# Feed-forward products of a pre-norm delta-rule block: seven-product float32 scheme replaced by two one-pass halves with integer weights, behind a check of the weights

## The chip, the core and the metric

The kernel runs on one core of one Trainium2 chip. The core has five engines that work side by side: TensorE (PE in the profile, with its weight loads shown apart as PEld), VectorE (DVE), ScalarE (ACT), GpSimd (POOL) and SyncE (SP), which here issues nearly all DMA transfers. The metric is the device time of one execution in microseconds (us). The kernel before takes 2001.05 us, the median of three runs (1995.74 to 2001.29).

## The reference

32 sequences of 512 tokens with 256 features, float32. A layer norm is followed by the attention block (a second layer norm, keys normalised to unit length, a triangular solve with the keys' Gram matrix, an answer from queries and keys, then an MLP with ReLU), and that by a gated feed-forward block whose weights are int32 numbers times 1/127. Only the last part is changed:

```python
def _L0_ffn_ref(x, w_gate, w_up, w_down):        # x: 32 x 512 x 256
    SCALE = 1.0 / 127.0
    wg = w_gate.astype(x.dtype) * SCALE          # 768 x 256, integers from -127 to 127
    wu = w_up.astype(x.dtype) * SCALE            # 768 x 256
    wd = w_down.astype(x.dtype) * SCALE          # 256 x 768
    gate = jnp.einsum('bsd,hd->bsh', x, wg)
    up = jnp.einsum('bsd,hd->bsh', x, wu)
    h = jax.nn.silu(gate) * up
    return jnp.einsum('bsh,dh->bsd', h, wd)
...
x = x + _L0_attn_ref(_layernorm(x), ...)
x = x + _L0_ffn_ref(_layernorm(x), w_gate, w_up, w_down)
```

## The kernel before

**Pairs and phases.** The 32 sequences are worked on in 16 pairs; in the code a pair is `one, two`. The order of every engine's instructions is the order in which the Python program emits them (`tc.manual_schedule`), so an instruction that waits holds up everything behind it on its engine. In the steady state the program goes round three phases, and each works on up to three pairs at once:

- the **values phase** (`values_phase`) of the newest pair: `gather` (tile `pf`), `through_values` (`pz`), `through_keys` (`pm`), `answer` (`po_d`), the layer norm `normed(s, "m")`. Beside it VectorE runs the inversion of the next pair's diagonal blocks (`invert`, lines 770 and 776), dealt out in small steps: each TensorE operation calls `spend(columns)`, and that moves each generator in `sides` on at its own rate;
- the **middle** (`middle`) of the pair before: the MLP (`mlp_in`, tile `pa`, line 1013; `mlp_out`, `po_m`, line 936), the layer norm `normed(s, "f")`, and between them the first steps of the newest pair's solve (`solution`: `merge` with tiles `pw` and `py`, then `solve` with `pr` and `pu`). `merge` starts with three VectorE transposes of the inverted blocks, which come back through DRAM (`found`, then `yb`, lines 785 and 791);
- the **gated phase** (the loop over `gated(old)`): the gate and up products of the feed-forward block for the pair before, the rest of the solve, the input norm of the next pair (`prepare`, which ends with a transpose by way of DRAM, `way_a` and `ag`, lines 502 to 515), and, from step `EARLY` on, the next pair's keys (`pk`, line 623) and Gram matrices (`pg`, line 665).

A transposed tile of a norm takes four DMAs out (`Turn.send`, line 509) and one back (`Turn.fetch`, line 515), all on SP's queue, in the order of the program.

**The feed-forward products.** Each is done by blocks of two by two in seven products in place of eight (a Strassen scheme in the form with few additions). `Unit` holds one pair of 128-row blocks of gate or up: seven float32 matmuls of 128x256 (line 1069) with weights that were combined once at the start (`wgS`, `wuS`, seven blocks for each of three pairs), with inputs combined by `mixed` on GpSimd (`hS`, line 1041). Results are put together by ScalarE copies (lines 1083, 1091, 1103), VectorE (1121, 1132, 1140) and GpSimd (1109, 1110, 1115, 1136). `Down` does the last product for half a sequence: three products at once (`plain`, `po_x`, line 1200), a recombination of the hidden values on GpSimd (`mix`, lines 1223 to 1226), then four more (`combined`, `po_y`), all of 128x128. `plain` and `combined` of a pair are spread over the values phase and the middle that follow its gated phase. A float32 product is two MATMUL instructions in the trace.

**PSUM.** Eight banks: `ps_a` has three, `ps_x` one, and `ps_f`, from which the MLP, the values phase and the feed-forward products take theirs, four.

The constants at the head set where things stand in the gated loop of 85 steps:

```python
NORM, STORE, START, TURN, MIX, EARLY = 3, 8, 13, 15, 28, 56
PREPARE = 14 * 1024
INVERT = 17 * 1024
```

Of the kernel before, what the change touches and what calls it, by code (L numbers as in the profile page):

```python
# [11 lines left out]
I32 = mybir.dt.int32  # L12
AF = mybir.ActivationFunctionType
# [5 lines left out]
WSCALE = 1.0 / 127.0  # L19


@with_exitstack
def kernel(
    ctx: ExitStack,
    tc: tile.TileContext,
    x: bass.AP,
# [28 lines left out]


# [10 lines left out]
    NORM, STORE, START, TURN, MIX, EARLY = 3, 8, 13, 15, 28, 56  # L67
    BEGIN = 17
    PREPARE = 14 * 1024
# [269 lines left out]
    NP = NH // 2  # L339
    wdS = const.tile([P, NP, 7, P], F32, name="wdS")  # L340

    wgS = const.tile([P, NP, 7, P], F32, name="wgS")
    wuS = const.tile([P, NP, 7, P], F32, name="wuS")

    class Dequant:
# [19 lines left out]
        def scale(self):  # L368
            for r0, m, wi in self.parts:
                nc.gpsimd.tensor_scalar(wi.bitcast(F32), wi, WSCALE, None, ALU.mult)  # L370

# [11 lines left out]
    class Stationary:  # L383


        def __init__(self, dst):
            self.dst = dst
            self.a21 = wk.tile([P, NP, P], F32, tag="fz", name="a21", bufs=4)

        def put(self, cc, r0, m, pt):  # L390
            dst, some = self.dst, slice(r0 // 2, (r0 + m) // 2)
            pt = pt.rearrange("p (j i r) -> p j i r", i=2, r=P)
            nc.scalar.copy(dst[:, some, cc, :], pt[:, :, 0, :])
            nc.scalar.copy(dst[:, some, 3, :] if cc else self.a21[:, some, :], pt[:, :, 1, :])
            if cc == NF - 1 and r0 + m == NH:
                b = lambda i: dst[:, :, i, :]
                two = lambda o, x, y, op: nc.gpsimd.tensor_tensor(o, x, y, op)
                two(b(4), self.a21, b(3), ALU.add)
                two(b(6), b(0), self.a21, ALU.subtract)
                two(b(5), b(4), b(0), ALU.subtract)  # L400
                two(b(2), b(1), b(5), ALU.subtract)

    class Combined:


        def __init__(self):
            self.b12 = wk.tile([P, NP, P], F32, tag="uv", name="b12", bufs=1)

        def put(self, cc, r0, m, pt):
            j, k = cc // 2, cc % 2  # L410
            nc.scalar.copy(wdS[:, j, k, :], pt[:, :P])
            nc.scalar.copy(wdS[:, j, 6, :] if k else self.b12[:, j, :], pt[:, P:])
            if cc == NH - 1:
                b = lambda i: wdS[:, :, i, :]
                minus = lambda o, x, y: nc.gpsimd.tensor_tensor(o, x, y, ALU.subtract)
                minus(b(5), self.b12, b(0))
                minus(b(3), b(6), b(5))
                minus(b(4), b(6), self.b12)
                minus(b(2), b(1), b(3))

# [613 lines left out]
    def mixed(s):  # L1034


        tag = {"tag": "ka"} if s.n % NS == 0 else {"tag": "blocks", "bufs": 1}
        hS = wk.tile([P, 4, T // 2], F32, name=f"hS_{s.n}", **tag)
        t1, t2, t3, t4 = [hS[:, i] for i in range(4)]
        block = lambda f, t: s.hT[:, f, t * (T // 2) : (t + 1) * (T // 2)]  # L1040
        minus = lambda o, x, y: nc.gpsimd.tensor_tensor(o, x, y, ALU.subtract)
        s.B = {
            1: block(0, 0), 2: block(1, 0), 3: block(1, 1), 4: t4, 5: t1,
            6: t2, 7: t3,
        }
        minus(t1, block(0, 1), block(0, 0))
        yield
        minus(t2, block(1, 1), t1)
        yield
# [3 lines left out]
        yield  # L1053

    class Unit:

# [120 lines left out]

    class Down:

# [526 lines left out]
```

## Time and profile before

| | |
|---|---|
| median of three runs | 2001.05 us |
| profiled execution, first to last instruction (span) | 1992.6 us |
| runs beyond that span (median; lowest run) | 8.5 us; 3.1 us |
| TensorE clock granted, mean | 0.997 of full speed |
| ACT busy | 873.0 us (44%), 2271 instructions |
| POOL busy | 1151.5 us (58%), 1556 instructions |
| DMA | 164.14 MB, mean 82 GB/s |
| gate and up products (`py`, `pz`, line 1069) | 2688 matmul instructions of 128x256 |
| down products (`po_x`, `po_y`, `po_z`, line 1200) | 2688 matmul instructions of 128x128 |
| starts of the values phases 1 to 14 | 200.3 us to 1771.1 us: 13 periods, mean 120.8 us |

The profile is one execution, with a row for each instruction. Busy time is the union of an engine's rows; a matmul's end is modelled, so the price of one in a stream is read from the distance of starts, not from its duration: 16 `pf` instructions of 128x256 start at 822.89 us and the next operation at 826.34, so each costs 0.216 us, while its row says 0.379.

### The profile page before, as it was taken

The page shows a single profiled execution, that of the slowest core. Times are in us where ns is not written, and L with a number is a line of the kernel's source. Part 1 is how long each engine was busy: PE and PEld are TensorE (multiplying, and loading weights), DVE is VectorE, ACT ScalarE, POOL GpSimd, SP SyncE. Part 2 cuts the span into 40 slices and gives each one's busy share as a digit, 9 for nine tenths or more (in the row PEclk, how much of TensorE's full clock was granted, in tenths as well). Part 3 has the DMA queues.
Part 4 walks back from the last instruction along what each step waited for, and adds up shares of the span by engine and source line. Part 5 has one row for each costly group of instructions (what it writes and reads, how often), then busy time and mean ns, then how long its engine had stood idle before and what let it go on. Part 6 is the DMA issues. An engine that isn't in the chain of part 4 may idle for free.

```text
span 1992.6 us, 31232 instructions
## 1 busy us (share of the span) xinstructions
PE 1955.4 (98%) x10286; PEld 1582.8 (79%) x10286; DVE 1337.8 (67%) x3873; ACT 873.0 (44%) x2271; POOL 1151.5 (58%) x1556
## 2 busy tenths in 40 slices
PE   7999999999999999999999999999999999999998
PEld 4667878878788787887878788787877878878888
DVE  6774875849668495784848758496684957758254
ACT  5345353453534435353453534535344353434543
POOL 3435764656555565664657645565555656646666
PEclk9999999999999999999999999999999999999999
DMA  5111242423424233241332324233242332413120
GB/s 151 39 35 44 74 117 51 133 64 82 117 59 112 67 104 86 63 120 53 104 86 74 116 56 130 68 78 116 59 112 67 103 87 63 128 45 103 43 64 22
DMA packets 248426, 164.14 MB, mean 82 GB/s; under 512 B 80929, under 2 KB 223912, under 8 KB 248264
## 3 DMA queue, kind: packets, MB, share of 16 engines
q1 hardware_dynamic: 247750, 161.61, 29.8%
q8 instruction: 82, 1.34, 0.3%
q14 instruction: 80, 0.66, 0.1%
q10 hardware_dynamic: 434, 0.39, 0.1%
q0 software_dynamic: 80, 0.14, 0.0%
HBM read 96.02 MB, written 66.06 MB: 81 GB/s over the span
## 4 chain that ended last, share of the span: by engine, by line
PE 77%; DVE 15%; DMA 3%; POOL 2%; issue 1%; ACT 1%; SPq 0%; DVEq 0%; ACTq 0%; POOLq 0%
PE po_y L1200 7%; PE pg L665 6%; PE pyup L1069 6%; PE pygate L1069 6%; PE pa L1013 5%; PE pk L623 5%; PE po_m L936 5%; PE po_x L1200 5%; PE po_d L936 5%; PE pr L874 4%; PE pzup L1069 4%; PE pf L895 4%; PE pzgate L1069 4%; PE pu L884 3%; PE pm L895 2%; PE pz L895 2%
## 5 line engine op out<-in xcount | busy, mean ns | idle before, releaser
L1109 POOL TENSOR_TENSOR v_up<-v_up,five_up 128x256 f32<-128x256 f32 x96 | 70.1, 730 | 217.0 <-ACT v_up L1083 216.9
L1200 PE MATMUL po_y<-wdS,hid 128*128 128x128 f32 x1512 | 180.6, 276 | 0.0
L1200 PEld LDWEIGHTS po_y<-wdS,hid 128*128 128x128 f32 x1512 | 177.3, 192 | 4.1 <-issue 1.0
L1132 DVE TENSOR_TENSOR top_up<-top_up,pzup 128x512 f32<-128x512 f32 x96 | 64.9, 676 | 164.1 <-PE pzup L1069 161.7
L1069 PE MATMUL pyup<-hS,wuS 128*128 128x256 f32 x576 | 172.8, 382 | 1.2
L1069 PE MATMUL pygate<-hS,wgS 128*128 128x256 f32 x576 | 171.5, 379 | 0.1
L665 PE MATMUL pg<-kT 128*128 128x256 f32 (+3 forms) x512 | 157.1, 433 | 0.1
L1140 DVE TENSOR_TENSOR hid<-top_gate,pzgate 128x512 f32<-128x512 f32 x96 | 64.6, 673 | 125.8 <-PE pzgate L1069 125.7
L1200 PEld LDWEIGHTS po_x<-wdS,hid 128*128 128x128 f32 x1152 | 138.4, 192 | 4.4 <-DVE hid L1136 1.2
L1200 PE MATMUL po_x<-wdS,hid 128*128 128x128 f32 x1152 | 138.9, 275 | 1.0 <-DVE hid L1136 1.0
L1115 POOL TENSOR_TENSOR hid<-v_gate,five_gate 128x256 f32<-128x256 f32 x96 | 69.9, 729 | 120.6 <-ACT v_gate L1083 120.6
L1069 PEld LDWEIGHTS pyup<-hS,wuS 128*128 128x128 f32 x576 | 106.7, 190 | 38.3 <-issue 13.4
L1069 PEld LDWEIGHTS pygate<-hS,wgS 128*128 128x128 f32 x576 | 108.7, 190 | 28.2 <-issue 13.6
L1136 POOL TENSOR_TENSOR hid<-hid,top_up 128x512 f32<-128x512 f32 x95 | 120.8, 1271 | 15.9 <-DVE top_up L1132 15.9
L936 PE MATMUL po_m<-w2s,act 128*128 128x256 f32 x512 | 123.6, 385 | 0.0
L623 PE MATMUL pk<-ag,wa 128*128 128x512 f32 x256 | 120.4, 595 | 1.7 <-ACT ag L485 0.9
L665 PEld LDWEIGHTS pg<-kT 128*128 128x128 f32 x512 | 91.9, 190 | 36.0 <-issue 12.9
L1013 PE MATMUL pa<-hT_m,w1s 128*128 128x512 f32 x256 | 118.8, 607 | 0.0
L895 PE MATMUL pf<-a,dp 128*128 128x256 f32 x512 | 115.6, 379 | 0.0
L1069 PE MATMUL pzup<-hT_f,wuS 128*128 128x256 f32 x384 | 114.5, 380 | 0.5 <-DVE a L1251 0.4
L1069 PE MATMUL pzgate<-hT_f,wgS 128*128 128x256 f32 x384 | 114.8, 381 | 0.0
L433 POOL TENSOR_TENSOR r_m<-ve_m,neghalf 128x4 f32<-128x4 f32 x32 | 32.7, 1023 | 139.8 <-DVE nmn_m L459 139.8
(273 smaller groups left out, 4882.0 us busy)
## 6 DMA issues: line engine op xcount, KB each, us to landing
a<-in_L_attn_x_dram SPq DMA_DIRECT2D x32, 512.0 KB, 4.6
x<-in_L_attn_x_dram SPq DMA_DIRECT2D x32, 512.0 KB, 4.0
way_m<-turn_m SPq DMA_DIRECT2D x120, 128.0 KB, 2.3
hT_m<-way_m SPq DMA_DIRECT2D x30, 512.0 KB, 3.7
out_dram<-a SPq DMA_DIRECT2D x60, 256.0 KB, 2.9
way_a<-turn_a SPq DMA_DIRECT2D x112, 128.0 KB, 2.3
ag<-way_a SPq DMA_DIRECT2D x28, 512.0 KB, 3.7
way_f<-turn_f SPq DMA_DIRECT2D x112, 128.0 KB, 2.4
```

Of the source, the lines that this page charges most:

```text
L623: nc.tensor.matmul(pk, lhsT=wa[:, f, ts(o, P)], rhs=s.ag[:, f, :], start=(f == 0), stop=(f == NF - 1),)
L665: nc.tensor.matmul(pg[:, :w], lhsT=s.kT[:, f, ts(j, P)], rhs=s.kT[:, f, j * P :], start=(f == 0), stop=(f == NF - 1),)
L874: nc.tensor.matmul(pr, lhsT=s.go[j][:, ts(i - j - 1, P)], rhs=p_[:, j, :], start=(j == 0), stop=(j == i - 1),)
L895: nc.tensor.matmul(s.pp[:, o, :], lhsT=lhs[:, c, ts(o, P)], rhs=rhs[:, c, :], start=(c == 0), stop=(c == nk - 1),)
L936: nc.tensor.matmul(self.po[:, c % 2, :], lhsT=src[:, ts(c, P)], rhs=self.w[:, f, :], start=(f == 0), stop=(f == self.nk - 1),)
L1013: nc.tensor.matmul(pa, lhsT=w1s[:, f, ts(o, P)], rhs=s.hT[:, f, :], start=(f == 0), stop=(f == NF - 1),)
L1069: nc.tensor.matmul(dst, lhsT=self.w[:, self.j, self.SLOT[i], :], rhs=self.s.B[i], start=first, stop=last, skip_group_check=True,)
L1109: nc.gpsimd.tensor_tensor(v, v, self.five, ALU.add)
L1115: nc.gpsimd.tensor_tensor(to, self.half(v), self.half(self.five), ALU.add)
L1132: nc.vector.tensor_tensor(self.top, self.top, self.z, ALU.add)
L1136: later(4, lambda: engine.tensor_tensor(natural(g), natural(g), grouped(flat(self.top)), ALU.mult))
L1200: nc.tensor.matmul(po[:, i, :], lhsT=self.A[block][:, j, :], rhs=wdS[:, j, slot, :], start=(j == 0), stop=(j == NP - 1),)
```

## The change

The constants, the weights and the halves. Weights stay integers (the multiplication by 1/127 becomes one by 1.0; `WSCALE` moves into the SiLU's scale and, squared, into the last addition). `float32r` (`FR`) is a type of the same four bytes. Inputs and hidden values are split into a rounded copy and what is left:

```diff
-    NORM, STORE, START, TURN, MIX, EARLY = 3, 8, 13, 15, 28, 56
-    PREPARE = 14 * 1024
+    NORM, TURN, SPLIT, EARLY = 2, 14, 24, 26
+    GATED, TAIL = 44, 12
+    PREPARE = 16 * 1024
...
+    W = FR if exact else F32
+    PARTS = 2 if exact else 1
+    wgT = const.tile([P, NF, HID], W, name="wgT")
...
+    def widest(sources):
...
+        for i, (r0, m, wi) in enumerate(parts):
+            wf = wi.bitcast(F32).rearrange("p r c -> p (r c)")
+            nc.vector.tensor_tensor_reduce(
+                out=wf, in0=wf, in1=wf, scale=1.0, scalar=0.0,
+                op0=ALU.mult, op1=ALU.max, accum_out=top[:, i : i + 1],
+            )
+        nc.vector.tensor_reduce(top[:, 0:1], top, axis=AX.X, op=ALU.max)
+        pt = ps_f.tile([P, 512], F32, tag="mm", name="pwide")
+        nc.tensor.transpose(pt[0:1, :P], top[:, 0:1], ident)
...
+        nc.vector.tensor_scalar(wide, most, EXACT * EXACT, None, ALU.is_gt)
...
+    def split(s, first, second):
...
+        parts = wk.tile([P, 2, NF, T], FR, tag="split", name=f"split_{s.n}")
+        for f in range(NF):
+            nc.scalar.copy(parts[:, 0, f, :], s.hT[:, f, :])
+        for f, engine in enumerate((first, second)):
+            engine.tensor_tensor(
+                parts[:, 1, f, :], s.hT[:, f, :], parts[:, 0, f, :], ALU.subtract
+            )
```

`mixed`, `Unit` and `Down` go; `Block` (128 rows of the hidden values of one sequence) takes their place. The down product of a block adds to two PSUM banks that stay taken over a sequence's six blocks:

```diff
+        def project(self, w, name):
+            po = ps_f.tile([P, 512], F32, tag="mm", name=f"p{name}_{self.name}")
+            for p, part in enumerate(self.s.parts):
+                for f in range(NF):
+                    nc.tensor.matmul(
+                        po, lhsT=w[:, f, ts(self.j, P)], rhs=part[:, f, :],
...
+                    if f == NF - 1 or not exact:
+                        yield
+            return po
...
+            nc.scalar.activation(natural(self.h), grouped(pg), AF.Silu, scale=WSCALE)
...
+            nc.vector.tensor_tensor(h, h, grouped(pu), ALU.mult)
+            if exact:
+                mine = self.hid()
+                hi, lo = mine[:, 0, :], mine[:, 1, :]
+                later(2, lambda: nc.scalar.copy(hi, self.h))
+                later(3, lambda: nc.gpsimd.tensor_tensor(lo, self.h, hi, ALU.subtract))
...
+        def down(self, half_):
+            s, j = self.s, self.j
+            if j == 0:
+                s.po[half_] = ps_f.tile([P, 2, C], F32, tag="mm", name=f"po_f_{s.n}_{half_}")
+            po = s.po[half_]
+            for i in range(2):
+                for p in range(PARTS):
+                    nc.tensor.matmul(
+                        po[:, i, :], lhsT=self.mine[:, p, ts(2 * half_ + i, P)],
+                        rhs=wdT[:, j, :], start=(j == 0 and i == 0 and p == 0),
...
+            if j == NH - 1:
+                nc.vector.scalar_tensor_tensor(
+                    out=acc, in0=po, scalar=WSCALE * WSCALE, in1=acc,
+                    op0=ALU.mult, op1=ALU.add,
+                )
+                nc.sync.dma_start(
...
+                    acc,
+                )
...
+    LAG = 2
...
+        for n in range(len(blocks) + LAG):
+            if n < len(blocks):
+                for part in (blocks[n].gate, blocks[n].up):
+                    for _ in part(later):
+                        step()
+                        yield
+            if n >= LAG:
+                for half_ in range(NT // 2):
+                    blocks[n - LAG].down(half_)
+                    step()
+                    yield
```

The gated loop runs 44 of these 72 steps; 12 more go to the end of the next values phase, 12 to the middle, the last 4 behind them (`older` is the same generator). The middle and the values phase in the new order:

```diff
+        mlp_in(one, 0)
+        mlp_in(one, 1)
+        residual(one)
+        sides_[0].finish()
+        mlp_out(one, 0)
         step()
         mlp_out(one, 1)
         step()
+        some(older, TAIL)
+        normed(one, "f")
+        turned(two, "m")
+        whole(older)
+        step()
         mlp_in(two, 0)
         residual(two)
+        step()
         mlp_in(two, 1)
+        turned(one, "f")
         mlp_out(two, 0)
         step()
...
+        split(one, nc.vector, nc.gpsimd)
         mlp_out(two, 1)
         step()
...
         whole(gather(one))
         fetch_residual(one)
+        whole(gather(two))
+        fetch_residual(two)
+        biased(one)
         whole(through_values(one))
+        whole(through_values(two))
+        biased(two)
         whole(through_keys(one))
+        whole(through_keys(two))
         answer(one)
         normed(one, "m")
+        answer(two)
         turned(one, "m")
+        if following:
+            in_order(a)
+        some(older, TAIL)
+        normed(two, "m")
+        if following:
+            in_order(b)
+            sides_[1].finish()
```

The input norm of the next pair now starts with the gated loop, not at its step 13 (`prep = Side(prepare(following), 2 * 64, PREPARE)` ahead of the loop). The whole old entry point becomes `preln_delta_mlp_glu(..., exact, wide, ...)`; `widest` is called once, ahead of the first values phase, and the new entry point is:

```diff
+    wide = top.tile([1, 1], I32, name="wide")
+    preln_delta_mlp_glu(tc, True, wide, *args)
+    found = nc.values_load(wide[0:1, 0:1], min_val=0, max_val=1)
+    with tc.If(found > 0):
+        preln_delta_mlp_glu(tc, False, wide, *args)
```

The second body is the same program with `exact` false: float32 weights and no split. It runs when a weight's square exceeds 4096 squared; the weights here stay within 127.

## The prediction

> **What bounds the kernel now.** I read the page's engine shares first, then the chain that ended last, then one period engine by engine.
>
> ```profile
> PE 1955.4 (98%) x10286; PEld 1582.8 (79%) x10286; DVE 1337.8 (67%) x3873; ACT 873.0 (44%) x2271; POOL 1151.5 (58%) x1556
> ```
>
> ```profile
> PE 77%; DVE 15%; DMA 3%; POOL 2%; issue 1%; ACT 1%; SPq 0%; DVEq 0%; ACTq 0%; POOLq 0%
> ```
>
> TensorE is the bound. But the change takes work off it, so the question is what else is nearly as long. The stretches of one period (busy time of each engine; the first is a values phase, the second the first part of a middle) show it:
>
> ```profile
> 806.50:843.40 36.90, 36.90 (x241) 34.20 (x240) 32.54 (x102) 10.54 (x25) 26.34 (x30) 1.00 0.32 82
> 843.40:868.50 25.10, 25.10 (x155) 18.83 (x155) 21.31 (x57) 9.62 (x23) 14.72 (x20) 1.00 0.45 130
> ```
>
> In the values phase VectorE, third number, is busy for 32.5 of 36.9 us. The timelines of VectorE and SP there give the latencies behind it:
>
> ```profile
> 812.23 0.36 DVE L734 RECIPROCAL few<-blocks 128x32 f32<-128x32 f32 x1 [2.38 <-DMA blocks<-given]
> ...
> 829.54 1.55 DVE L502 STREAM_TRANSPOSE turn_m<-h_m 128x256 f32<-128x256 f32 x4
> ...
> 838.21 0.69 DVE L776 TENSOR_REDUCE beside<-xt 128x16 f32<-128x512 f32 x1
> ```
>
> ```profile
> 831.11 1.84 SPq L509 DMA_DIRECT2D way_m<-turn_m  x4
> 833.00 0.47 SPq L125 DMA_DIRECT2D x<-in_L_attn_x_dram  x1
> 835.22 0.38 SPq L515 DMA_DIRECT2D hT_m<-way_m  x1
> 839.34 0.34 SPq L785 DMA_DIRECT2D found<-xc  x1
> 841.06 0.36 SPq L791 DMA_DIRECT2D yb<-found  x1
> ```
>
> A transposed norm needs 4.2 us from VectorE's last transpose (831.0) to the fetch and 3.7 more to land (page, part 6): some 7.9 us. The inverted blocks need some 4.9 us from the last reduction (838.9) to `yb` on chip. Today the removed products are what TensorE does meanwhile.
>
> **TensorE, part by part.** Prices by distance of starts: f32 instruction of 128x256 0.216 us (16 `pf` in 3.45), of 128x128 0.1117 (18 `po_x` in 2.01). Removed: 2688 x 0.216 = 581, 2688 x 0.1117 = 300, together 881 us. Added: 32 x 48 = 1536 products of 128x512 and 1536 of 128x256 in `float32r`, which the trace doesn't have. Its bounds come from f32 rows: an f32 product of 128x512 (`pk`, four instructions in 1.72) costs 0.86 us; a quarter of it is 0.216, and of 128x256 0.108. I take the quarter: the kernel splits by hand what the f32 product shows as two instructions of doubled length. Loads keep up, as one per 0.112 us does in `po_x`. Sum: 332 + 166 = 498 us, so 383 us less, 24 per pair. At four quarters it would be 1992, at two 996.
>
> [...]
>
> A pair's work on TensorE is then, in the same prices, 25.9 us in the values phase (`pf` 6.9, `pz` 3.45, `pm` 3.45, `po_d` 6.9, 12 tail steps 5.2), 26.0 in the middle, 42.3 in the gated phase: 94 us, against 120.8 for a period.
>
> **The other engines.** VectorE loses lines 1132, 1140, 1121 and 1251 (64.9 + 64.6 + 39.1 + 87.8 = 256 us) and gains 192 products of 128x512 at 0.676 (130), 64 last additions at some 0.75 (48) and 16 splits (11): 67 less, 4 per pair, none of it in `invert`. GpSimd loses some 52 us of 72 per pair and gains 15 subtractions at 1.27 (19). ScalarE loses 29 and gains 17. Both are far from binding; GpSimd's `lo` is on the path once (below).
>
> **The path of a pair in the new order** (t from the start of its values phase).
>
> 1. `few` needs the next pair's Gram blocks, stored last thing: t = 5.7, as today (806.5 to 812.2). From there VectorE has in order: `invert` (19.05 us, from 812.23 to 838.9 less the 7.6 of others in it), both `m` (0.8), both `answer` with their statistics (7.2), four and four transposes (3.1), two tail products (1.3), and one wait of some 2.4: `normed(one)` now stands right behind `answer(one)`, so VectorE stands from 21.7 until GpSimd's `r_m` (1.02), `mr_m` and ScalarE's first `h_m`. It ends `invert` at 40.
> 2. hT_m of `one`: last transpose 25.6, on chip 33.5. TensorE has only 25.9 us of work and waits 7.6. Two MLP halves (6.9) end at 40.4.
> 3. `pw` needs `yb`: 40.1 + 4.9, then three transposes: 46.3. TensorE stands 6, and the 12 tail steps that could fill this are queued behind `pw`.
> 4. From `pw` to the gated loop: 19.1 us of TensorE. `lo` of the last tail block comes behind the four `h_f` on ScalarE, then 1.27 on GpSimd: 2.1 of wait. The fetch of hT_m of `two` stands behind four sends of f-norm of `one` on SP, whose transposes stand behind the last tail product: 2.5 more. Gated loop at 70.
> 5. In it the spend of 256 columns per step at rate 128/16384 brings the first `ag` fetch out at step 25, and step 26 asks for it. The last transpose stands behind the product of block 3 (step 18, TensorE at 15.6 us, VectorE some 3 behind): t = 90; send, fetch and landing 7.5 (890.98 to 898.4): `pk` at 97.5, TensorE there at 91. Today this wait is 0.8 us in all:
>
> ```profile
> PE pk L623 <- DMA ag<-way_a: 0.8, 1, 0.8
> ```
>
> 6. Then 23.5 us of pure TensorE (18 steps 7.8, `pk` 6.9, `pg` 8.6) to the next values phase: 121.
>
> **The clock.** At the one place where TensorE stands 2.9 us today, the granted clock (before the DMA share) falls to half:
>
> ```profile
> 109.20:112.00 2.80, 0.00 (x0) 0.00 (x0) 2.73 (x11) 0.62 (x2) 1.24 (x2) 0.98 0.00 0
> 112.00:114.60 2.60, 2.52 (x8) 1.48 (x8) 2.57 (x9) 2.03 (x4) 0.00 (x0) 0.50 0.00 0
> 114.60:117.00 2.40, 2.40 (x5) 1.17 (x4) 2.37 (x10) 0.59 (x2) 0.83 (x1) 0.50 0.00 0
> ```
>
> Eight `pa` there take 5.5 us, not 3.45: 2.1 us lost. Of the waits above, those of 3 and 5 have critical work right behind: 2 x 2.1 = 4.2, so 125.2 per period, bounds 121 and 130 (each wait at the 3.9 that `tp_m` and `pa` lose together there).
>
> [...]
>
> **The ends.** `widest` is 4608 elements per partition on VectorE (1.22 per 1024, L1005: 5.5) with its small steps, and a TensorE transpose waits for it: +6, bounds 0 and 8. First gated phase: 62 to 53, -9. Gated phase 14, without `pk` and `pg`, -6. From the last values phase: 117.6 now; 25.9 + 4 + 6.9 + 7 + 2 + 9 + 72 steps 31.2 + 4 for the last halves + 3 for the store, clock 4: 97; register load and branch have no row, bounds 0 and 12 (the first DMA wait), taken 5, by the landing of a small load (3.6): 102, -15. Together -24.
>
> **Sum.** 13 x (125.2 - 120.8) = +57, -24: +33 on the span of 1992.6, 2026, and 2034 with the 8.5 us by which the median stands above it. Own range 1995 to 2110.
>
> **Rivals.**
>
> - *The path is shorter.* For it: sums of VectorE alone give `pw` at 43.4, the two waits of 4 vanish, VectorE keeps step with TensorE in 5, and a period is 114, with one clock fall 116: -62 and -24, some 1915 (1860 to 1990). It decides below 122.6 per period, where the 24 us of the ends outweigh the rest. Against it: each wait follows from the order of one queue.
> - *TensorE stays the bound:* 94 + 2.8 (today's 120.8 less 118 of work) = 97 per pair, 2001 - 309 - 24, about 1668. It needs some 25 us of waits per pair to go, and nothing in the order covers them.
> - *The product is not one pass*, or its loads don't hide: two quarters add 31 us per pair, some of it inside the waits: 128 at least, I take 140: about 2250, with nothing won at the ends. From some 1.9 quarters on (96.8 + 0.9 x 31) TensorE itself is longer than the path.
>
> **Chances.** Path of 125: 0.52 (of it 0.05 within 0.3%); shorter path 0.35; TensorE-bound 0.04; not one pass 0.09. About 0.3% (6 us) is what a measurement of this kernel can tell from no change. Faster 0.39, same 0.05, slower 0.56. The range leaves out the TensorE-bound case, the shorter path's low end and most of the last case: 1895 to 2115.
>
> **What would show it.** Right: TensorE near 75 to 80%, gate and up products of 0.22 us, waits of `pa` on hT_m, `pw` on `xparts` and `pk` on `ag` of 5 to 8 us per pair, the clock at half behind them, VectorE dense through the values phase. Wrong: TensorE over 90% busy, or `ag` landed before step 26, or products dearer than 0.3 us.

## The result, and the profile after

The changed kernel takes 2155.31 us (median of four runs, 2148.24 to 2161.57) against 1998.73 us for the kernel before in the same comparison (1995.74 to 2001.29): a ratio of 1.078, 95% interval 1.0745 to 1.081. The forecast was 2034 us, slower by 33; it became slower by 157. The profiled execution has a span of 2146.4 us.

The engine shares and the chain that ended last, from the page of the changed kernel:

```profile
PE 1761.5 (82%) x7983; PEld 1307.6 (61%) x7983; DVE 1254.4 (58%) x3597; ACT 703.3 (33%) x1525; POOL 623.9 (29%) x837
...
PE 42%; DVE 26%; DMA 19%; SPq 4%; issue 4%; ACT 3%; POOL 2%; DVEq 0%; POOLq 0%; ACTq 0%
```

TensorE was busy for 98% and is now for 82%, its granted clock is 0.906 of full speed on average against 0.997, and it holds 42% of the chain where it held 77%. It lost work and the kernel got longer: DMA, at 3% of the chain before, now has 19%. What TensorE waits for (engine, line, releaser: us in total, times, longest):

```profile
PE pk L608 <- DMA ag<-way_a: 128.1, 28, 6.8
PE po_f L1089 <- ACT hf L1060: 71.5, 15, 5.2
PE pa L998 <- DMA hT_m<-way_m: 49.0, 14, 3.8
PE pup L1046 <- DVE hf L1065: 26.3, 15, 1.8
PE pw L801 <- DVE xparts L796: 19.8, 15, 2.4
...
PE pwide L402 <- DVE widest L400: 6.0, 1, 6.0
```

`pk` waits 28 times, that is twice per pair; before it waited 0.8 us in all. The starts of the values phases 1 to 14 are 198.7 to 1935.0 us: 13 periods of 133.6 us on average, against 120.8. That is 13 x 12.73 = +165.5 us; from values phase 14 to the end the kernel takes 211 us against 222, so -10, and values phase 1 starts 1.6 us earlier: +154 in all, as the spans differ (2146.4 - 1992.6).

One period, 603.59 to 736.26 us, from the timeline of TensorE (start, duration, operation, and in brackets the idle time before it):

```profile
632.21 2.07 PE L1089 MATMUL po_f<-wdT,hid 128*128 128x256 f32 x8 [5.16 <-ACT hf L1060]
...
651.78 1.15 PE L801 MATMUL pw<-xparts,gs 128*64 128x64 f32 x16 [1.20 <-DVE xparts L796]
...
667.10 3.75 PE L998 MATMUL pa<-hT_m,w1s 128*128 128x512 f32 x4 [3.48 <-DMA hT_m<-way_m]
707.55 3.78 PE L608 MATMUL pk<-ag,wa 128*128 128x512 f32 x4 [6.58 <-DMA ag<-way_a]
727.00 1.98 PE L608 MATMUL pk<-ag,wa 128*128 128x512 f32 x4 [2.71 <-DMA ag<-way_a]
```

The windows of the same period (stretch, length, busy time of PE, PEld, DVE, ACT and POOL with instruction counts, granted clock, DMA share, GB/s):

```profile
632.20:642.40 10.20, 7.68 (x24) 6.09 (x25) 9.96 (x27) 2.71 (x6) 5.21 (x5) 0.50 0.35 90
...
662.50:679.60 17.10, 13.49 (x77) 8.66 (x77) 7.18 (x15) 3.44 (x9) 1.57 (x2) 0.80 0.46 138
679.60:700.80 21.20, 21.12 (x104) 17.22 (x102) 18.90 (x58) 10.66 (x22) 10.52 (x17) 1.00 0.20 53
...
707.50:714.70 7.20, 7.14 (x15) 3.73 (x16) 0.00 (x0) 1.47 (x3) 0.12 (x1) 0.68 0.00 0
```

In each of the three long waits (5.16, 3.48, 6.58) the granted clock falls, at 630.17, 664.30 and 705.26 us, and the work behind them starts at the lower clock, 0.50 until 643.83, 671.13 and 712.09. VectorE is busy for 10.0 of 10.2 us in the first stretch, where TensorE runs at half clock, and for nothing in the last.

The price of a product is read from the distance of starts: four `pgate` instructions of 128x512 take 0.93 to 0.94 us, so 0.234 each, and eight `po_f` of 128x256 take 0.94, so 0.1175 each. Each of these one-pass products is one MATMUL instruction in the trace (1536 rows of each shape), where an f32 product is two; that one costs 0.86 us at 128x512 (`pk`) and 0.43 at 128x256 (`pf`). So the new price is 0.27 of the f32 price, for each some 8% above the quarter of the forecast.

### The profile page after: what moved, and what is told of

Its sections match the earlier page's. It is cut to its first block, busy times and chain, and to the rows that moved or that the text cites. A ratio compares the mean times of both kernels' runs of the same rounds, so it can differ in the third digit from the quotient of the medians.

```text
span 2146.4 us, 24418 instructions
## 1 busy us (share of the span) xinstructions
PE 1761.5 (82%) x7983; PEld 1307.6 (61%) x7983; DVE 1254.4 (58%) x3597; ACT 703.3 (33%) x1525; POOL 623.9 (29%) x837
## 4 chain that ended last, share of the span: by engine, by line
PE 42%; DVE 26%; DMA 19%; SPq 4%; issue 4%; ACT 3%; POOL 2%; DVEq 0%; POOLq 0%; ACTq 0%
PE pk L608 6%; PE pup L1046 5%; DMA ag<-way_a 5%; PE pgate L1046 5%; PE pa L998 5%; DVE xt L755 4%; PE pr L859 4%; PE pg L650 4%; SPq L494 4%; DMA hT_m<-way_m 3%; DMA blocks<-given 3%; DVE beside L761 3%; PE po_f L1089 3%; PE po_m L921 3%; DMA way_a<-turn_a 3%
## 5 line engine op out<-in xcount | busy, mean ns | idle before, releaser
L1089 PE MATMUL po_f<-wdT,hid 128*128 128x256 f32 x1536 | 265.4, 315 | 94.6 <-ACT hf L1060 71.5
L1070 POOL TENSOR_TENSOR hid<-hf,hid 128x512 fp32r<-128x512 f32 x192 | 244.9, 1281 | 325.4 <-ACT hid L1069 325.4
L1065 DVE TENSOR_TENSOR hf<-hf,pup 128x512 f32<-128x512 f32 x192 | 130.8, 682 | 349.6 <-PE pup L1046 304.8
L1089 PEld LDWEIGHTS po_f<-wdT,hid 128*128 128x128 f32 x1536 | 232.8, 209 | 134.9 <-ACT hf L1060 78.0
L1046 PE MATMUL pgate<-split,wgT 128*128 128x512 f32 x768 | 267.1, 459 | 12.5 <-DVE a L927 10.1
L1046 PE MATMUL pup<-split,wuT 128*128 128x512 f32 x768 | 254.9, 444 | 26.3 <-DVE hf L1065 26.3
L608 PE MATMUL pk<-ag,wa 128*128 128x512 f32 x256 | 149.1, 715 | 129.0 <-DMA ag<-way_a 128.1
L1046 PEld LDWEIGHTS pup<-split,wuT 128*128 128x128 f32 x768 | 153.1, 202 | 82.9 <-DVE hf L1065 36.8
L1060 ACT ACTIVATE hf<-pgate 128x512 f32<-128x512 f32 x192 | 114.4, 596 | 206.1 <-PE pgate L1046 140.2
L1046 PEld LDWEIGHTS pgate<-split,wgT 128*128 128x128 f32 x768 | 146.0, 204 | 55.4 <-DVE a L927 14.4
L1069 ACT CAST hid<-hf 128x512 fp32r<-128x512 f32 x192 | 118.6, 618 | 179.4 <-DVE hf L1065 178.7
L650 PEld LDWEIGHTS pg<-kT 128*128 128x128 f32 x512 | 88.6, 190 | 44.7 <-issue 16.8
```

What stands on the lines that cost most here:

```text
L608: nc.tensor.matmul(pk, lhsT=wa[:, f, ts(o, P)], rhs=s.ag[:, f, :], start=(f == 0), stop=(f == NF - 1),)
L650: nc.tensor.matmul(pg[:, :w], lhsT=s.kT[:, f, ts(j, P)], rhs=s.kT[:, f, j * P :], start=(f == 0), stop=(f == NF - 1),)
L1046: nc.tensor.matmul(po, lhsT=w[:, f, ts(self.j, P)], rhs=part[:, f, :], start=(p == 0 and f == 0), stop=(p == PARTS - 1 and f == NF - 1),)
L1060: nc.scalar.activation(natural(self.h), grouped(pg), AF.Silu, scale=WSCALE)
L1065: nc.vector.tensor_tensor(h, h, grouped(pu), ALU.mult)
L1069: later(2, lambda: nc.scalar.copy(hi, self.h))
```

## The experiments

**Theory:** the time of the changed kernel is set by the chain of VectorE's work, round trips by DMA and waits, in the order of the queues; the removed work of TensorE was cover for it. **Rivals:** TensorE's own work or the price of its new products sets the time; the second body and its branch cost. Each comparison is with the kernel before on the same chip; a period is the mean of the 13 from values phase 1 to 14 in the profiled execution.

| run | edit | us, median | period |
|---|---|---|---|
| changed kernel | | 2155.3 | 133.6 |
| e1 | no branch, no second body | 2155.4 | 133.9 |
| e2 | general float32 body alone | 2358.3 | 145.9 |
| e3 | keys behind the gated loop | 2108.4 | 130.0 |
| e4 | low halves left out | 2106.1 | 131.2 |
| e5 | hT_m fetched first | 2094.6 | 129.5 |
| e6 | input norm begun in the middle | 2011.3 | 122.3 |
| e7 | 40 products added per pair | 2119.1 | 130.8 |
| e8 | e5 and e6 | 1928.1 | 117.1 |
| e9 | inversion finished ahead of the tail | 2229.1 | 139.2 |
| e10 | e8, tail dealt out, inversion finished early | 1970.1 | 119.6 |
| e11 | load of the next input later | 2154.3 | 133.7 |
| e12 | e8 and e11, keys denser | 1919.4 | 116.0 |
| e13 | e9, copy of the inversion on VectorE | 2208.1 | 137.4 |
| e14 | e12, aT copies behind the tail | 1922.2 | 116.6 |

### e1: without the branch

```diff
     preln_delta_mlp_glu(tc, True, wide, *args)
-    found = nc.values_load(wide[0:1, 0:1], min_val=0, max_val=1)
-    with tc.If(found > 0):
-        preln_delta_mlp_glu(tc, False, wide, *args)
```

> The register load, the branch and the whole second body are taken out; the search for the widest weight stays. Waits theory (the time is set by the in-order chain of VectorE, the round trips by DMA and the waits they put into TensorE's queue): the branch costs only what stands behind the last store, 0 to 12 us less, so 2143 to 2155 us, and a period of the values phases stays at 133.5. Rival (the second body in the program costs while the first runs, for instance in fetching instructions): the periods get shorter, 13 x 5 us or more, so 2090 or below.

Measured 2155.44 us (2148.14 to 2163.57), ratio to before 1.0793 [1.0751, 1.0836], a period of 133.9. The second body costs the periods nothing that can be measured. At the end, where 5 us had been allowed, the medians scatter too much to tell, but the two traces differ: the last store starts 99.3 us into the last values phase in both, and the execution ends 8.1 us after that start in the changed kernel and 3.3 us after it in e1 (6.8 in e3, which has the branch). So the register load and the branch cost some 3.5 to 4.8 us there.

### e2 and e4: more and less work for TensorE

```diff
-    preln_delta_mlp_glu(tc, True, wide, *args)
-    found = nc.values_load(wide[0:1, 0:1], min_val=0, max_val=1)
-    with tc.If(found > 0):
-        preln_delta_mlp_glu(tc, False, wide, *args)
+    preln_delta_mlp_glu(tc, False, wide, *args)
```

> Only the general body: same order, same steps, but gate, up and down as one float32 product each with unrounded inputs, so no split and no hi and lo. By the f32 rows (0.86 us for 128x512, 0.43 for 128x256) the products are 768 x 0.86 + 768 x 0.43 = 991 us against 538 now, +453 us or 28 per pair. Waits theory: the waits that TensorE has per pair (some 21 us of idle time, and the slow clock behind them) take up most of it, a period of 137 to 142, about 2225 us (2180 to 2280). Rival (TensorE's own work sets the time): 2155 + 453, about 2610. If it is near 2155, the one-pass products are worth nothing in this order.

Measured 2358.32 us (2347.04 to 2362.56), ratio 1.1796 [1.175, 1.1841]: above the theory's range, far below the rival's. 28 us more work per pair lengthen the period by 12.4. So the waits took up somewhat over half of it, not most; with 91% busy time TensorE is near the bound again there.

```diff
-                for p in range(PARTS):
+                for p in range(1):
                     nc.tensor.matmul(
                         po[:, i, :], lhsT=self.mine[:, p, ts(2 * half_ + i, P)],
```

(and the same in `project`)

> The products of the low halves are left out of gate, up and down (the output lacks these terms); the split, the copies, the subtractions and all steps stay. That takes 269 of the 538 us of these products from TensorE, 16.8 per pair. Waits theory: what lies in the tail of the values phase and ahead of pk becomes waiting time, and only the steps behind pk (3.9 us) and those behind pw (2.6 us) are on the path: 2 to 8 less per period, 2050 to 2130 us, TensorE's waits on ag, hT_m and hf longer. Rival (the price of the products sets the time): 2155 - 269, about 1886.

Measured 2106.07 us (2098.81 to 2114.21), ratio 1.0549 [1.0507, 1.0592]. 16.8 us per pair taken from TensorE shorten the period by 2.4. The rows of what it waits for then:

```profile
PE pk L608 <- DMA ag<-way_a: 151.2, 27, 8.0
PE po_f L1090 <- ACT hf L1061: 84.6, 15, 5.9
PE pa L998 <- DMA hT_m<-way_m: 70.9, 14, 6.2
```

All three have grown, together by 58 us. Over the whole execution TensorE's idle time (span less busy time) is 544 us against 385, and its granted clock 0.857 against 0.906: of the 269 us of work that go, some 160 come back as waiting and some 60 as work at the lower clock, an estimate from the busy times (1555.8 us against 1761.5). The price of the products doesn't set the time, and the 8% by which they were dearer can't explain 121 us.

### e3 and e6: the wait of `pk` on the input norm

```diff
-    NORM, TURN, SPLIT, EARLY = 2, 14, 24, 26
+    NORM, TURN, SPLIT, EARLY = 2, 14, 24, 44
```

> One constant: EARLY 26 -> 44, so the keys and the Gram matrices of the next pair stand behind the 44 steps of the gated loop and not between them. Waits theory: the 18 steps that follow step 26 (7.8 us) run while the input norm's round trip ends, so both waits of pk on ag (6.6 and 2.7 us per period) and the slow clock behind the first (2.3 us) go: 9 to 11.6 less per period, 122 to 124.5, and 13 periods make it 2005 to 2035 us. Rival (TensorE's work or product price sets the time): no work is removed, so at most 1% less, 2135 to 2155. Rival (the wait only moves): the wait is found again in front of pk or in the next values phase, and the period falls by under 4 us.

Measured 2108.41 us (2100.44 to 2113.97), ratio 1.0558 [1.0516, 1.0599]; 3.5 us per period, a third of what the theory said. The third possibility is what happened. TensorE and VectorE of e3 in one period that begins at 591.96:

```profile
697.84 3.60 PE L608 MATMUL pk<-ag,wa 128*128 128x512 f32 x8
701.28 4.56 PE L650 MATMUL pg<-kT 128*128 128x512 f32 x16
711.81 5.38 PE L608 MATMUL pk<-ag,wa 128*128 128x512 f32 x8 [5.97 <-DMA ag<-way_a]
```

```profile
694.96 0.41 DVE L542 CUSTOM_DVE_ANT_0 a<-a,beside 128x256 f32<-128x256 f32 x1
695.30 0.08 DVE L542 DVE_READ_ACCUMULATOR2_ANT left<- 128x1 f32 x1
695.49 0.17 DVE L568 COPY beside<-rr 128x4 f32<-128x4 f32 x1
698.30 0.48 DVE L570 SCALAR_TENSOR_TENSOR a<-a,left,beside 128x255 f32<-128x255 f32 x1 [2.65 <-POOL left L549]
```

The first `pk` no longer waits, the second waits 5.97 us: the second sequence's norm was itself late, and on VectorE it stood 2.65 us for a small GpSimd step that was queued behind the subtractions of `lo`. Waiting later doesn't help where the norm comes last; it has to start earlier:

```diff
         whole(older)
+        if following:
+            following[0].prep = Side(prepare(following), 2 * 64, PREPARE)
         step()
         mlp_in(two, 0)
...
-                    prep = Side(prepare(following), 2 * 64, PREPARE)
+                    prep = following[0].prep or Side(prepare(following), 2 * 64, PREPARE)
```

> The input norm of the next pair is set going in the middle, right behind the last tail products, where VectorE stands idle for several stretches of 2 to 7 us, and not with the gated loop; its rate and EARLY stay. Waits theory: its transposes no longer stand behind VectorE's products of the gated loop, both waits of `pk` on ag (6.6 and 2.7 us) and the slow clock behind them (2.3) go: 9 to 11.6 less per period, 122 to 124.5 and 2005 to 2035 us. If run e3 fell short because the second sequence's norm was late, this one must not fall short. Rival (the round trip itself or TensorE's work sets it): under 4 us per period, 2105 or above.

Measured 2011.32 us (2006.5 to 2013.69), ratio 1.0081 [1.0063, 1.01], a period of 122.3: as the theory had it. No work was taken away, only the moment of the norm was moved, and the excess over the kernel before falls from 157 to 15 us. The waits of e6:

```profile
PE pa L999 <- DMA hT_m<-way_m: 48.4, 15, 3.8
...
PE pk L609 <- DMA ag<-way_a: 4.3, 2, 3.9
```

`pk` on `ag` fell from 128.1 us to 4.3; the wait on hT_m is as it was.

### e5 and e8: the fetch of hT_m, and both moves

```diff
+        turned(two, "m")
         some(older, TAIL)
         normed(one, "f")
-        turned(two, "m")
         whole(older)
```

> One line moved: the fetch of hT_m of `two` is issued ahead of the tail products and the f-norm of `one` in the middle, so that on SP's queue it no longer stands behind that norm's four sends. Nothing else changes. Waits theory: the wait of `pa` on hT_m (3.5 us per period) goes and with it the slow clock behind it (some 2.5 us): 3.5 to 6 less per period, 127.5 to 130, and 2075 to 2110 us. Rival (the wait only moves): what comes next is set by something else, `pk` waits longer for ag by as much, and the time stays within 1% of 2155.

Measured 2094.63 us (2090.31 to 2097.54), ratio 1.0492 [1.0469, 1.0515], a period of 129.5: within the theory's range, and the wait falls from 49.0 us to 0.4.

> The moves of e5 and e6 together. Waits theory: 13 to 17 less per period, 116.5 to 120.5, so 1930 to 1990 us, which is at or under the kernel before. If both act on the same slack, the time is that of the better of the two alone.

Measured 1928.09 us (1923.05 to 1930.53), ratio 0.9652 [0.9632, 0.9672]: faster than the kernel before by 3.5%, and 2 us below the range given. The period fell by 16.5 us, where the two moves alone gave 4.1 and 11.2: they act on different stretches and add up.

### e7: work added where TensorE waits

```diff
+    def warm(n):
+        pd = ps_a.tile([P, 512], F32, tag="mm", name=f"warm_{len(warmed)}")
+        warmed.append(n)
+        for i in range(n):
+            nc.tensor.matmul(
+                pd, lhsT=wgT[:, 0, :P], rhs=wgT[:, 1, : 512],
+                start=(i == 0), stop=(i == n - 1),
+            )
...
+        warm(14)
         mlp_in(two, 0)
...
+                    if i == EARLY and tail_:
+                        warm(26)
```

> Work is added: 14 one-pass products of 128x512 into an unread PSUM tile ahead of `pa` of `two` in each middle, and 26 ahead of the first `pk` in the gated loop, 40 x 0.233 = 9.3 us per pair, 130 us in all; their results are used by nothing. They fill the two longest of TensorE's waits on the path. Waits theory with the clock: they cost nothing, since TensorE waited there, and the clock no longer falls behind those waits, so 0 to 4.8 us less per period: 2090 to 2155 us. Rival (TensorE's work sets the time): +130 us, 2285. If the time stays at 2155 to 2165, the fall of the clock cost nothing on the path.

Measured 2119.07 us (2113.8 to 2127.09), ratio 1.0625 [1.059, 1.0659]: 36 us faster with some 9 us more work per pair. From the timeline of e7:

```profile
659.39 3.47 PE L1209 MATMUL warm<-wgT 128*128 128x512 f32 x14
...
694.85 6.07 PE L1209 MATMUL warm<-wgT 128*128 128x512 f32 x26
701.56 1.98 PE L608 MATMUL pk<-ag,wa 128*128 128x512 f32 x4 [0.63 <-DMA ag<-way_a]
```

The first four `pk` instructions now have 1.98 us where they had 3.78: they run at full clock (1.00 from 694 to 712 us). hT_m comes no earlier (its `pa` starts 15.4 us after `pw`, 15.3 in the changed kernel), and `pk` 1.9 us sooner after it, as `pa` and `pw` behind the wait take 3.0 us and not 4.9. So what is won, 2.7 us per period, is the clock's share of the two waits. It is an account of the slow clock alone, and a lower one, since the second wait of `pk` (2.77 us here) stays, and in 8 of the 13 periods the `pk` behind it now run slower (last section).

### e9, e13, e10: the values phase, where two attempts made it longer

```diff
         if following:
             in_order(a)
+            sides_[1].finish()
+            next(sides_[0].gen)
         some(older, TAIL)
         normed(two, "m")
         if following:
             in_order(b)
-            sides_[1].finish()
-            next(sides_[0].gen)
```

> In the changed kernel the rest of the inversion and the fetch of its result (`found`, `yb`) are issued ahead of the values phase's tail products and of the m-norm of `two`, so `found` no longer stands behind that norm's four sends on SP, nor the last reductions behind its four transposes on VectorE. Nothing else changes. If `pw` is late only because of that queue, it starts 2 to 4 us earlier in every period: 2105 to 2130 us. If TensorE itself reaches `pw` no earlier, because the tail products before it stall (5.2 us on the SiLU behind other ScalarE work, then half clock), only its wait there of 1.3 us goes: 0 to 1.5 per period, 2135 to 2155.

Measured 2229.14 us (2225.75 to 2244.08), ratio 1.1177 [1.1131, 1.1222]: neither answer; 74 us slower than the changed kernel. `found` was sent 40.5 us into the phase, not 41.8, yet `pw` came at 55.1 and not at 48.2. ScalarE and TensorE of e9 show why (the phase begins at 620.63):

```profile
660.76 0.37 ACT L768 COPY xc<-beside 128x256 f32<-128x256 f32 x1 [11.27 <-DVE beside L761]
661.03 0.62 ACT L1069 CAST hid<-hf 128x512 fp32r<-128x512 f32 x1
661.55 0.60 ACT L1060 ACTIVATE hf<-pgate 128x512 f32<-128x512 f32 x1
```

```profile
662.21 2.07 PE L1046 MATMUL pgate<-split,wgT 128*128 128x512 f32 x4 [7.68 <-ACT hf L1060]
```

The inversion's result is copied by ScalarE. Moved ahead, that copy waits 11.27 us for VectorE's last reduction, the tail's SiLU stands behind it, and TensorE waits 7.68 us for the SiLU to free a PSUM bank.

```diff
-        (nc.scalar.copy if g > NS else nc.vector.tensor_copy)(done, xc)
+        nc.vector.tensor_copy(done, xc)
```

> e9 with one engine changed: the copy of the finished inversion (`xc`) is done by VectorE and not by ScalarE. In e9 ScalarE stood 11.3 us at that copy until VectorE's last reduction, and the tail's SiLU stood behind it. If that queue is what cost e9 its 74 us, the SiLU now comes some 11 us earlier and TensorE's wait of 7.7 us on it goes; the product of the tail's first block still stands behind the inversion on VectorE, so not all is won back: 2155 to 2200 us. If the order on VectorE alone is the cause, it stays at 2229.

Measured 2208.14 us (2204.46 to 2211.3), ratio 1.1053 [1.1032, 1.1074], 8 us above the range given: ScalarE's queue is 21 of the 74 us. The rest fits VectorE's order: in e13 TensorE waits 6.47 us in one period for a `pup` bank, whose product now stands behind the whole inversion, and 91.1 us in all for such banks, against 26.3 in the changed kernel. No run undoes that order alone.

For e10, four tail steps were put ahead of `answer(one)` and four behind it, on top of e8, and the inversion finished as in e9:

```diff
+        some(older, 4)
         answer(one)
+        some(older, 4)
         normed(one, "m")
...
-        some(older, TAIL)
+        some(older, TAIL - 8)
```

> On top of e8: the 12 tail steps of the values phase are dealt out as four ahead of the answer of `one`, four behind it and four at their old place, and the inversion's end and its fetch are issued ahead of the last four (as in e9). The SiLU then stands ahead of the normalisations on ScalarE's queue, so the 5.1 us wait of `po_f` and the half clock behind it go, and `found` is sent earlier. Waits theory: `pw` 3 to 5 us earlier in each period, a period of 111 to 113.5 against 116.4, so 1865 to 1893 us. Rival (the inversion is as late, since VectorE now has the tail's products in its way): `pw` where it was, within 1% of 1928.

Measured 1970.14 us (1963.39 to 1977.35), ratio 0.9863 [0.9829, 0.9897]: 42 us slower than e8, against both answers. The waits suggest why. The tail's two `po_f` banks stay taken over the six blocks; with them held from before the answers on, `po_d`, `pgate` and `pup` share what is left of `ps_f` and wait for VectorE one by one (`pgate`, `pup` and `po_f` on VectorE's answer: 25.4, 24.3 and 19.7 us in all). It also has e9's copy in it, so the shares aren't told apart, and no run tests the banks by themselves.

### e11, e14: two small pieces, and e12

```diff
-                if following and g + 2 < n_pairs:
-                    load_a(pairs[g + 2][0])
...
         whole(gather(two))
         fetch_residual(two)
+        if following and following[0].n + NS < N:
+            load_a(pairs[following[0].n // NS + 1][0])
```

> In the changed kernel one load is moved: the 512 KB load of the input two pairs ahead stands on SP between the Gram blocks' stores and the fetch of `blocks`; here it stands behind the residual loads of the values phase. The changed kernel's `few` starts 8.3 us after the values phase, where the kernel before has 5.7 (the fetch issued 3.4 after, not 1.8, and landing in 4.85, not 3.9). If that load is the cause, `few` starts at 5.7 to 6.5, and `pw` up to 2.6 earlier: 2120 to 2150 us, the low end if TensorE reaches `pw` early enough, the high end if its stalls in the tail hold it. If `few` stays at 8.3, the load isn't the cause.

Measured 2154.34 us (2148.45 to 2157.41), ratio 1.0784 [1.0764, 1.0805]: no effect on the time. `few` starts at 7.3 instead of 8.3 us (611.21 in a phase that begins at 603.93), so the load is 1.0 of the 2.6 us, by a landing of 3.8 and not 4.85; the fetch is issued as late as before (3.5). `pw` comes at 47.4 and not at 48.2; over the 13 periods, at 47.5 and not at 48.9 on average. But from `pw` to the gated loop it then takes 28.9 us and not 27.8, and from the first `pk` to the next values phase 29.6 and not 29.1: what is won ahead of `pw` is lost behind it.

For e12 the last key and Gram steps also come sooner, on top of e8 and e11:

```diff
-                    if i >= EARLY and i % 2 == 0 and solved:
+                    if i >= EARLY and (i % 2 == 0 or i >= 38) and solved:
```

> e8 with e11's move, and from step 38 of the gated loop one key or Gram step behind every step and not every second, so that the last Gram block is stored some 1.4 us sooner. Waits theory: the inversion begins 3 to 4 us earlier against the values phase and `pw` follows by 1.5 to 3.5: a period of 113 to 115 against 116.4, 1883 to 1910 us. If TensorE's own order in the tail holds `pw`, it stays within 0.5% of 1928.

Measured 1919.41 us (1915.63 to 1929.18), ratio 0.9621 [0.9596, 0.9645], a period of 116.0: the best of all, but its interval overlaps e8's, and the 1883 to 1910 expected were not reached. The time lies where the other answer put it (within 0.5% of 1928), but not for its reason: `pw` does come 1.9 us earlier than in e8 (47.3 and not 49.1 on average), and 0.85 of that is lost on the way from `pw` to the gated loop.

For e14 the two `aT` copies are moved, on top of e12:

```diff
         turned(one, "m")
-        if following:
-            in_order(a)
         some(older, TAIL)
+        if following:
+            in_order(a)
         normed(two, "m")
```

> e12 with the two ScalarE copies that put aT of the next pair's first sequence in order (1.1 us) moved behind the values phase's tail products, so that the tail's SiLU stands 1.1 us earlier on ScalarE. If TensorE's stall there holds `pw`, 0.5 to 1.1 us per period: 1904 to 1914. If VectorE's inversion holds it, no change: within 4 us of 1919.

Measured 1922.2 us (1917.08 to 1924.09), ratio 0.961 [0.9589, 0.963]: no change against e12, as the answer that VectorE's inversion holds `pw` had it. TensorE's stall in the tail fell by 1.1 us (4.1 for 5.2, the longest wait of `po_f` on `hf`), but its waits of `pgate` on VectorE's `a` grew from 10.2 to 20.3 us in all, and those before `pw` from 24.7 to 26.4.

Why a shorter tail alone wins nothing can be seen in rows of VectorE of the changed kernel:

```profile
648.89 0.69 DVE L934 TENSOR_TENSOR a<-a,po_m 128x512 f32<-128x512 f32 x1 [3.02 <-PE po_m L921]
649.62 0.75 DVE L435 BATCH_NORM_STATS2 bnst_f<-a 128x6 f32<-128x256 f32 x2
650.29 0.30 DVE L437 BATCH_NORM_AGGREGATE bnmv_f<-bnst_f 128x2 f32<-128x6 f32 x2
650.84 0.43 DVE L795 STREAM_TRANSPOSE xparts<-yb 32x256 f32<-32x256 f32 x1 [0.26 <-DMA yb<-found]
```

The transposes that `pw` needs stand on VectorE behind the addition of `po_m`, which TensorE gives late because of its tail, and wait for `yb`, which the inversion gives late. VectorE is ready 0.26 us before `yb` lands (0.5 on average over the 13 periods, 0.7 in e12): two chains that end close together, the inversion's a little later. Shortening the tail alone can't bring `pw` forward then, which fits e14. e11 did bring it forward; why the gain is lost behind `pw` was not followed further. No run shortened both chains without adding a new wait, so what both together are worth stays open.

## Why the forecast was too low

**Right.** Slower, and for the reason given: TensorE goes from bound to waiting (82% busy, forecast 75 to 80), and `pk` on `ag`, `pa` on hT_m and `pw` on `xparts` are among its waits, though with 9.2, 3.5 and 1.3 us per pair where 5 to 8 had been given. `widest` makes TensorE wait the 6.0 us that were forecast. The first wait on `ag` was forecast to start 21 us into the gated loop and to last 6.5: in the period shown it starts 21.4 us in and lasts 6.58. The quarter was near, an estimate of the author's that no row of before shows: 0.234 against 0.86 us. The "doubled length" of an f32 instruction is 0.43 against 0.234 at 128x512, so 1.84 times.

**Wrong.** The period: 133.6 and not 125.2, which is 13 x 8.36 = 109 of the 121 us; the ends are the other 12. By the steps of the forecast, in the period shown and on average over the 13:

| step | forecast | period shown | mean of 13 |
|---|---|---|---|
| 1: `few`; `invert` ends | 5.7; 40 | 8.3; 41.2 | 9.0; 41.9 |
| 2: TensorE has done the MLP halves | 40.4 | 47.0 | 47.4 |
| 3: `pw` | 46.3 | 48.2 | 48.9 |
| 4: from `pw` to the gated loop | 23.7 | 27.8 | 27.8 |
| 5: from there to `pk` | 27.5 | 27.9 | 27.8 |
| 6: from `pk` to the next values phase | 23.5 | 28.7 | 29.1 |
| slow clock, booked apart | 4.2 | in 4 and 6 | in 4 and 6 |

The four last steps on the path are on average 2.6 + 4.1 + 0.3 + 5.6 = 12.6 us longer, of which 4.2 had been allowed for the clock: 8.4 too little.

- *Step 6, "Then 23.5 us of pure TensorE", is the one that failed most.* It followed one sequence's norm. The second sequence's transposes stand on VectorE behind its product of block 5 (counted from 0), whose `pup` stands on TensorE behind the very `pk` that waits: the wait on `ag` delays the next one. VectorE and SP between the two waits:

```profile
714.96 0.69 DVE L1065 TENSOR_TENSOR hf<-hf,pup 128x512 f32<-128x512 f32 x1 [10.77 <-PE pup L1046]
...
718.92 0.45 DVE L487 STREAM_TRANSPOSE turn_a<-a 128x256 f32<-128x256 f32 x1
```

```profile
719.40 1.83 SPq L494 DMA_DIRECT2D way_a<-turn_a  x4
723.35 0.38 SPq L500 DMA_DIRECT2D ag<-way_a  x1
```

The wait returns with 2.71 us, and the slow clock behind the first one is in this step too. e3 and e6 show it from both sides: letting the first wait be filled moved it to the second sequence, an earlier start of both norms removed 11.2 us per period. In e6 the stretch of step 6 takes 23.4 us on average, which is the forecast's 23.5 with hardly any wait in it.
- *Step 4: the wait on the fetch was under-sized, and the clock behind it left out.* 2.5 us was forecast, 3.48 measured, as the fetch lands 5.1 us after its issue and not 3.8; the allowance for the clock was given to the waits of 3 and 5, not to this one. e5 gives 4.1 per period back.
- *Step 2 was wrong in kind, at little cost.* "TensorE has only 25.9 us of work and waits 7.6" took the 12 tail steps at 5.2 us. They take 17.6 (624.84 to 642.45): the SiLU stands on ScalarE behind four `h_m` and two `aT` copies, and from 630.2 on the stretch runs at half clock. ScalarE there:

```profile
628.04 2.08 ACT L449 ACTIVATE h_m<-a,mr_m,r_m 128x256 f32<-128x256 f32 x4 [10.01 <-POOL mr_m L446]
630.02 1.12 ACT L625 COPY aT<-ag 128x512 f32<-128x512 f32 x2
631.05 0.61 ACT L1069 CAST hid<-hf 128x512 fp32r<-128x512 f32 x1
631.57 0.58 ACT L1060 ACTIVATE hf<-pgate 128x512 f32<-128x512 f32 x1
```

hT_m, fetched at 634.61, was there when `pa` came. So a second chain ended together with the one that was forecast, and `pw` lost 1.9 us, not 7; but it is this tail that e9, e10 and e14 ran into.
- *Step 1* took 5.7 us from the phase before. There the stores of the Gram blocks began 1.2 us before the values phase, here 0.5 after it (604.08), and a moved load lengthens the landing (4.85 us, 3.8 without it in e11). Less waiting on VectorE later made up for most of it.
- *The ends:* -11.7 and not -24. From the last values phase to the end it takes 107.4 us (102 forecast), the gated phase before it saves nothing where 6 had been counted, the start 1.6 of 3.
- *The price* of 0.216 was 8% low. By e4 (2.4 us per period for 16.8 us of work) the 2.5 us per pair that this makes are worth some 0.4 us per period, an estimate.
- *Small slips in the sums:* the terms of step 1 add up to 39.6 and not 40, those of step 6 to 23.3 and not 23.5, and two waits at 3.9 make the upper bound of the period 128.8 and not 130. None of them explains the miss.

**The rivals.** Not one pass: two quarters would be 0.43 us at 128x512, and the rows have 0.234. TensorE-bound at 1668: e4 leaves out half of these products and takes 2106. The shorter path, 1915: what failed was its condition, that VectorE keeps step by itself. e8, with the waits on hT_m and `ag` removed by moves, takes 1928, but by another path: its `pw` comes at 49.1 us on average and not at 43.4, and the norm starts earlier than in the rival's order. That the two numbers are near is luck.

## What to carry to other kernels

When an engine that covered everything loses a fifth of its work, price the order of the queues, not the work: follow every round trip for every sequence of the pair, and ask of each wait what is queued behind it that the next wait needs. A wait is removed by starting its producer earlier (e6: -144 us without any work saved), not by asking for it later (e3: a third of the hoped). Before moving a step ahead, list what it issues on every engine: e9's move was for SP's queue, and it cost 74 us, 21 of them by one copy on ScalarE (e13) and the rest, as far as the waits tell, by one product on VectorE.

## What the runs showed of the hardware

The fall of the granted clock doesn't follow from the length of one wait. Two waits of the same `pk` in nearly the same place, in the changed kernel and in e7:

```profile
724.30:727.00 2.70, 0.00 (x0) 0.00 (x1) 0.00 (x0) 0.22 (x1) 0.30 (x1) 1.00 0.81 219
727.00:729.00 2.00, 2.00 (x5) 1.04 (x6) 0.00 (x0) 0.00 (x0) 0.00 (x0) 1.00 0.00 0
```

```profile
716.00:718.90 2.90, 0.13 (x2) 0.02 (x1) 0.00 (x0) 0.34 (x1) 0.41 (x1) 0.88 0.68 203
718.90:721.00 2.10, 2.10 (x3) 1.07 (x4) 0.00 (x0) 0.00 (x0) 0.00 (x0) 0.50 0.04 8
```

After 2.71 us the clock stays at 1.00, after 2.77 us it is 0.50. Over 13 periods, the clock is at 1.00 when the second wait of `pk` ends every time in the changed kernel (2.71 to 4.08 us); behind one of them, the longest, it falls 0.67 us later. In e7 the four `pk` behind the second wait take longer than the 1.98 to 1.99 us of full clock in 8 of 13 periods (2.45 to 3.78 us, behind waits of 2.74 to 3.23), yet 1.98 behind the longest wait, 3.69. One difference between the two is what came before: in the changed kernel's period the clock has been back at 1.00 for only some 12 us when this wait begins (from 712.09 to 724.29); in e7, where the first wait is filled, it is at 1.00 in all that was read ahead of it from 657 us on (657 to 676, 694 to 716). That this is the reason is not shown.

In the changed kernel's period the low stretches last 6.83 us around the waits on hT_m and `ag` (664.30 to 671.13, 705.26 to 712.09), where dense work follows, and 13.66 in the tail of the values phase (630.17 to 643.83), where the work comes in pieces between waits. The stretches at 1.00 between them last 20.47 and 34.13 us. All of these are whole multiples of 3.41 us, which is the length of the shortest low stretch in this trace (800.84 to 804.25). In e7 the clock falls at 718.2, 2.1 us after the wait had begun, and rises at 725.0.

That a one-pass product of 128x512 costs 0.234 us, where one of the two instructions of an f32 product of 128x256 costs 0.216, stays unexplained.
